# FFN weights transposed on TensorE instead of in a DMA, with a new order of VectorE's work beside the attention steps

## The chip, the cores and the metric

The kernel runs on one core of a Trainium2 chip. The metric is the device time of one execution in microseconds (us). Five engines work side by side, each through its own list of instructions in program order: TensorE (PE in the profile; its weight loads are PEld), VectorE (DVE), ScalarE (ACT), GpSimd (POOL) and SyncE (SP), which here only issues DMAs. They wait for one another on semaphores. TensorE writes into PSUM, of which this kernel uses eight banks of 128 x 512 float32.

## The reference

For each of four sequences of 512 rows and 512 columns, `x + s * g` is computed. `xn` is the layer norm of x. `s` is causal attention on xn with 16 heads of 32 columns; q and k get an RMS norm and a rotary embedding. `g` is silu of a gated FFN on xn with 1408 hidden columns, whose weights are integers less a zero point, times a scale for each row:

```python
def _qlinear(x, wq, scale):
    W = (wq.astype(jnp.float32) - ZERO_POINT) * scale[:, None]      # ZERO_POINT = 128
    return jnp.einsum('bsd,hd->bsh', x, W)

xn = _layernorm(x)
s = attention(xn, w_qkv, w_out, q_gamma, k_gamma)                   # 16 heads, causal
gate = silu(_qlinear(xn, wq_gate, s_gate))                          # wq_gate, wq_up: 1408 x 512
up = _qlinear(xn, wq_up, s_up)
g = silu(_qlinear(gate * up, wq_down, s_down))                      # wq_down: 512 x 1408
x = x + s * g
```

## The kernel before, in words

There is no scheduler: the order in which the Python code calls the instructions is the order on each engine. Work goes in 16 units (b, g): sequence b from 0 to 3, group of four heads g from 0 to 3. A unit has two stages.

`hidden_window` computes a chunk of the FFN: two 128-column pieces f in g = 0, three in the others. For each piece `hidden` makes the gate and the up product (16 matmuls of 512 columns; xn is split into two float32r halves, `xh` and `xl`), `gate` and `gated` apply silu and scales. Between them stand, as `fills`, leftovers of the unit before: its last attention step, and `fresh.turn`, which transposes the queries and keys of this unit on TensorE (tile `qkt`, L422).

The second stage is attention. A `Step` t handles queries t*128 to t*128+127: `scores` on TensorE (tile `sc`, L452), `probabilities` (for each of four heads a minimum on VectorE, L473, and an exponential on ScalarE, L483), a transpose of the result, and `values` (L539). Beside it run: the contraction of the FFN chunk with w_down (`contract`, `contract_two`, tile `dn`), the projections of the next unit (`fresh.product`, tile `qkv`, L370) and their rotation (`fresh.rotate`: `square` on ScalarE with the copy of v, three multiplications and a sum on VectorE, L402 to L409, then four operations on GpSimd, L410 to L412, the first being the sum qk + qs).

The stage has two forms. `attention_window` (units (0,0) to (0,2)) transposes the probabilities on TensorE (tile `pt`, L499). `placed_window` (the 12 units (0,3) to (3,2)) transposes them in 32 x 32 blocks on VectorE (`blocks`, L521) and puts these in place with four DMAs on SP (`spread`). In `placed_window` of g = 0 the output products of the sequence before are made too (`result.project`, tile `so`, L678, and `result.finish`), and q of the next unit's first tile is projected early, into a bank of the other pool. In g = 3 the next sequence's xn is split into halves: `norm.cut(t)` rounds on ScalarE (L352) and subtracts on GpSimd or VectorE (L353).

PSUM pools, in rings: `bank_a` has four banks (scores, qkv, h, so), `bank_t` two (transposes, one dn, some qkv and h), and one each hold `pv` and `dn`. A tile of a ring is free once its last reader is done.

The integer weights (34 pieces, 128 x 512 or 128 x 384) are prepared during units (0,0) to (0,2), two in each call of `weights()`: a load on SP (L247), a cast to bfloat16 on ScalarE (L256), a DMA transpose on SP (L258), and on VectorE the zero point's subtraction into float32r with a running maximum (L265). `weights()` is called behind each piece f of `hidden_window` and four times in each `attention_window`. `prologue` prepares the first four pieces. The pieces lie in `rooms`, memory that is used for other things later.

Of the kernel before, what the change touches and what calls it, by code (L numbers as in the profile page):

```python
# [13 lines left out]
BF16 = mybir.dt.bfloat16  # L14
U32 = mybir.dt.uint32
I32 = mybir.dt.int32
AF = mybir.ActivationFunctionType
ALU = mybir.AluOpType
# [3 lines left out]
P = 128  # L22
# [3 lines left out]
NT = N // P  # L26
NC = D // P
# [5 lines left out]
ZERO_POINT = 128.0  # L33
# [18 lines left out]
def interleaved(  # L52
# [27 lines left out]
    nc = tc.nc  # L80
# [23 lines left out]
    def bank_t(name):  # L104
        return ps_t.tile([P, 512], F32, tag="t", name=name)
# [37 lines left out]
    ident = const.tile([P, P], F32, name="ident")  # L143
# [41 lines left out]
    def load_scales():  # L185
# [5 lines left out]
            at += n  # L191
        return srow, at

    sdown = const.tile([P, D], F32, name="sdown")

    def prepare_scales(srow, at):
        tp = bank_t("sps")
# [32 lines left out]
    todo = list(preparations())  # L230
    n_prep = len(todo)
    largest = const.tile([P, n_prep], F32, name="largest")
    loaded, turning, finished = [], [], set()

# [2 lines left out]
    now = [0]  # L239
# [7 lines left out]
                nc.sync.dma_start(raw.bitcast(U32), src.bitcast(U32))  # L247
                loaded.append((now[0], room, raw, k, dst, name))

    def turn_weights():  # L250


        _, room, raw, k, dst, name = loaded.pop(0)
        halves_ = raw.bitcast(BF16)
        n = k * P
        nc.scalar.copy(halves_[:, :n], raw.bitcast(U32))  # L256
        turned = halves_[:, n:].rearrange("p (c r) -> p c r", r=P)
        nc.sync.dma_start(turned, halves_[:, :n], transpose=True)  # L258
        turning.append((now[0], room, turned, k, dst, name))

    def finish_weights():

        _, room, turned, k, dst, name = turning.pop(0)
        i = len(finished)
        nc.vector.tensor_scalar(  # L265
            dst,
            turned,
            -ZERO_POINT,
            None,
            ALU.add,  # L270
            ALU.max,
            accum_out=largest[:, i : i + 1],
        )
        if len(finished) >= NC:
            rooms.append(room)
        finished.add(name)

    def weights(n=2):

        now[0] += 1  # L280
        for _ in range(n):
            if turning and now[0] - turning[0][0] >= 2:
                finish_weights()
        load_weights(n)
        for _ in range(n):
            if loaded and now[0] - loaded[0][0] >= 1:
                turn_weights()

    def find_wide():

# [69 lines left out]
    class Projection:  # L360
# [16 lines left out]
            self.banks[t] = bank  # L377

        def square(self, t):
            bank = self.banks[t]  # L380
            nc.scalar.activation(squares, bank[:, : 2 * P], AF.Square)  # L381
            nc.scalar.copy(self.v[:, t, :], bank[:, 2 * P :])  # L382

        def rotate(self, t, squared=False):


            bank = self.banks[t]
            name = f"{self.b}_{self.g}_{t}"
            if not squared:
                self.square(t)  # L390
            qk = qp.tile([P, 2 * P], F32, tag="qk", name=f"qk_{name}")
            qs = tp_.tile([P, 2 * P], F32, tag="qs", name=f"qs_{name}")

            def four(a):
                return a.rearrange("p (i h d) -> p i h d", i=2, d=HD)

            def table(k, cols):
                a = tab[:, t, :, k, cols]
                return a.unsqueeze(2).to_broadcast([P, 2, HPG, a.shape[-1]])

            bank4 = four(bank[:, : 2 * P])
            nc.vector.tensor_tensor(four(qk), bank4, table(0, slice(0, HD)), ALU.mult)  # L402
            for lo, hi in ((0, half), (half, 0)):
                lo, hi = slice(lo, lo + half), slice(hi, hi + half)
                nc.vector.tensor_tensor(  # L405
                    four(qs)[:, :, :, lo], bank4[:, :, :, hi], table(1, lo), ALU.mult
                )
            ss = small.tile([P, 2 * HPG], F32, tag="ss", name=f"ss_{name}")
            nc.vector.tensor_reduce(ss, heads(squares), AX.X, ALU.add)  # L409
            nc.gpsimd.tensor_tensor(qk, qk, qs, ALU.add)  # L410
            inverse_root(ss, ss, HD * RMS_EPS)
            nc.gpsimd.tensor_tensor(  # L412
                heads(qk), heads(qk), ss.unsqueeze(2).to_broadcast([P, 2 * HPG, HD]), ALU.mult
            )
            self.qk[t] = qk
# [15 lines left out]
    class Step:  # L431
# [79 lines left out]
        def blocks(self, *js):  # L511

            n = self.t + 1
            used = HPG * self.keys
            probs = piece(self.first, n)[:, :used].rearrange("p (m k c) -> p c m k", c=4, k=32)
            way = piece(self.way, n)[:, :used].rearrange("p (c m k) -> p c m k", c=4, k=32)
            for j in js[:: self.per]:
                blocks = slice(j * n, (j + self.per) * n)  # L520
                nc.vector.transpose(way[:, :, blocks], probs[:, :, blocks])  # L521
# [302 lines left out]
    def placed_window(b, g, last, s, fresh, norm, result):  # L824

        def halves(engine, *tiles):
            if norm is not None:
                for t in tiles:  # L830
                    norm.cut(t, engine)

        def beside(t):
            if result is not None:
                result.project(t)
                result.finish(t)

        def load(*tiles):
            if result is not None:
                for t in tiles:  # L840
                    result.load(t)

        def values():
            for t in range(NT - 1):
                s[t].values()

        load(0)
        s[0].scores()
        s[1].scores(s[0].whole, s[0].keys)
        s[0].probabilities(0, 1, 2, 3)  # L850
        if g == 0:
            fresh.product(0, other=True)
            fresh.square(0)
        adds = contract_two(b, g)
        s[1].probabilities(0, 1, 2, 3)
        adds[0]()
        if g == 0:
            fresh.rotate(0, squared=True)
        if last.placed:
            last.values()  # L860
        s[2].scores()
        adds[1]()
        if g == 0:
            last.divide()
        s[0].blocks(0, 1, 2, 3)
        s[0].spread()
        s[2].probabilities(0, 1, 2, 3)
        add = contract(b, g, 2)
        s[2].blocks(0, 1, 2, 3)
        s[2].spread()  # L870
        if g:
            fresh.product(0)
            fresh.rotate(0)
        s[1].blocks(0, 1, 2, 3)
        s[1].spread()
        load(1, 2)
        if g == 0:
            add()
        halves(nc.gpsimd, 0, 1)
        for t in range(NT):  # L880
            if t:

                fresh.product(t, other=t == NT - 1 or (g > 0 and t == NT - 2))
                fresh.rotate(t)
            if t == 1 and g:
                add()
                last.divide()
            if t == 1:
                halves(nc.vector, 2, 3)
            beside(t)  # L890
            if t == 1:
                load(3)
        if g == 0:
            values()
        s[3].scores()
        s[3].probabilities(0, 1, 2, 3)
        contract(b, g, 3)()
        if g:
            values()
# [67 lines left out]
    def prologue():  # L967
        norm, fresh = Norm(0), Projection(0, 0)
        load_weights(4)
        scales_in = load_scales()  # L970
        load_weights(4)
        for t in range(NT):
            norm.stats(t)
            norm.roots(slice(t, t + 1))
            if t:
                norm.apply(t - 1)
                norm.turn(t - 1)
        norm.apply(NT - 1)
        prepare_table()
        norm.cut(0, nc.vector)  # L980
        norm.cut(1, nc.vector)
        fresh.product(0)
        fresh.rotate(0)
        norm.turn(NT - 1)
        norm.cut(2, nc.vector)
        norm.cut(3, nc.vector)
        load_weights(3)
        for _ in range(4):
            turn_weights()
        fresh.product(1)  # L990
        fresh.rotate(1)
        for _ in range(4):
            turn_weights()
        for t in range(2, NT):
            fresh.product(t)
            fresh.rotate(t)
            finish_weights()
            finish_weights()
        load_wqkv(slice(1, 2))
        now[0] += 1  # L1000
        prepare_scales(*scales_in)
        return fresh

    fresh, last, norm, done = prologue(), None, None, None
    for u, (b, g) in enumerate(units):
# [17 lines left out]
                done.store(t)  # L1023
        if (b, g) == (0, NC - 1):
            next(finding)
            nc.sync.dma_start(wout, w_out.rearrange("(c p) m -> p c m", p=P))
        if b == 0 and 2 + g < NC:
            load_wqkv(slice(2 + g, 3 + g))
        if (b, g) == (0, 0):
            nc.sync.dma_start(sdown, s_down.partition_broadcast(P))  # L1030
        if (b, g) == (0, NC - 2):
            finding = find_wide()
            next(finding)
# [485 lines left out]
```

## Time and profile before

| | |
|---|---|
| three runs, us | 658.75, 659.25, 659.99 (median 659.25) |
| profiled execution, us | 656.71, of which 654.9 are the span from first to last instruction |
| mean granted TensorE clock | 0.992 |
| busy, share of the span | PE 95%, DVE 74%, ACT 53%, POOL 48% |
| DMA transposes | 34, on SP |
| attention stage of (2,0) begins | 342.83 us (first `sc`) |
| attention stage of (2,1) begins | 393.11 us |

In the profile a line such as `PE so L678 <- DVE least L473: 6.6, 3, 2.2` says that TensorE's products `so` waited for VectorE's `least` for 6.6 us in all, three times, 2.2 us the longest. In a timeline the first two numbers are start and duration in us, `x8` is the number of instructions merged into the line, and brackets give the idle time before it and what ended that. `PEclk` is the share of full speed that TensorE was granted. The three units (1,0), (2,0) and (3,0) are alike, and so are (0,3), (1,3) and (2,3).

### The profile page before, as it was taken

What the parts mean: (1) busy time and instruction counts of PE and PEld (TensorE: products, weight loads), DVE (VectorE), ACT (ScalarE), POOL (GpSimd) and SP (SyncE); (2) the same over time, 40 slices, a digit from 0 to 9 for tenths busy, and PEclk for the clock granted to TensorE, in tenths of its full rate; (3) what the DMA queues carried; (4) which work ended last, traced back from release to release, by engine and by line L of the source; (5) the groups of instructions that cost most, each with busy time, mean ns of one, the idle gap of its engine ahead of it and who ended that gap; (6) DMA issues with size and microseconds to landing.
All of it is one profiled execution on the core that took longest, in us unless ns stands there. A gap on an engine that the chain in (4) does not pass through costs nothing.

```text
span 654.9 us, 11673 instructions
## 1 busy us (share of the span) xinstructions
PE 622.2 (95%) x3906; PEld 413.7 (63%) x3906; DVE 482.4 (74%) x1248; ACT 346.3 (53%) x895; POOL 317.0 (48%) x365
## 2 busy tenths in 40 slices
PE   4989999999988999999998999999997999999995
PEld 3646757667564576758664476767765467676752
DVE  4677776755988479797998369799798657969553
ACT  2666765646473264546755046464756136464560
POOL 3925235352563626544382633637194442727422
PEclk9999999999999999999998999999999899999999
DMA  8594853100433146243323425523233505333401
GB/s 267 144 215 110 185 133 101 66 1 1 98 82 87 59 130 162 66 96 66 79 44 81 121 48 144 137 61 83 65 80 82 145 1 146 82 73 89 130 1 70
DMA packets 65584, 62.63 MB, mean 96 GB/s; under 512 B 22998, under 2 KB 48876, under 8 KB 65516
## 3 DMA queue, kind: packets, MB, share of 16 engines
q1 hardware_dynamic: 64556, 61.38, 37.7%
q8 instruction: 33, 0.54, 0.3%
q10 hardware_dynamic: 960, 0.43, 0.2%
q14 instruction: 35, 0.29, 0.1%
HBM read 21.80 MB, written 4.19 MB: 40 GB/s over the span
## 4 chain that ended last, share of the span: by engine, by line
PE 79%; DVE 12%; ACT 4%; issue 2%; DMA 2%; POOL 0%; DVEq 0%; ACTq 0%
PE h L585 22%; PE qkv L370 21%; PE so L678 9%; PE sc L452 5%; PE dn L632 5%; PE dn L615 5%; PE pv L539 5%; DVE arena L521 3%; PE pt L499 2%; DVE arena L473 2%; PE qkt L422 2%; DVE qs L405 1%; PE rt L563 1%; ACT arena L483 1%; PE xnt L346 1%
## 5 line engine op out<-in xcount | busy, mean ns | idle before, releaser
L370 PE MATMUL qkv<-wqkv,xnT 128*128 128x384 f32 x512 | 172.5, 490 | 2.3 <-DVE least L473 2.3
L483 ACT ACTIVATE arena<-arena,least 128x128 f32<-128x128 f32 (+3 forms) x256 | 140.6, 551 | 63.4 <-DVE least L473 63.2
L370 PEld LDWEIGHTS qkv<-wqkv,xnT 128*128 128x128 f32 x512 | 96.3, 191 | 69.0 <-issue 4.2
L521 DVE STREAM_TRANSPOSE arena<-arena 128x512 f32<-128x512 f32 (+1 forms) x132 | 126.1, 1002 | 0.0
L410 POOL TENSOR_TENSOR qk<-qk,qs 128x256 f32<-128x256 f32 x64 | 48.2, 753 | 156.0 <-DVE qs L405 156.0
L473 DVE CUSTOM_DVE_ANT_0 arena<-sc,mask 128x128 f32<-128x128 f32 (+3 forms) x256 | 109.3, 485 | 15.1 <-PE sc L452 13.8
L604 POOL TENSOR_TENSOR h<-sil,h 128x512 fp32r<-128x512 f32 x44 | 57.9, 1315 | 110.5 <-ACT h L603 110.5
L317 POOL TENSOR_TENSOR ss<-ss,minus_half 128x8 f32<-128x8 f32 x64 | 106.9, 1671 | 5.3
L381 ACT ACTIVATE squares<-qkv 128x256 f32<-128x256 f32 x64 | 24.5, 383 | 122.5 <-PE qkv L370 98.0
L602 DVE SCALAR_TENSOR_TENSOR sil<-h,scales,sil 128x512 f32<-128x512 f32 x44 | 32.7, 743 | 52.6 <-PE h L585 43.7
L678 PE MATMUL so<-wout,oT 128*128 128x512 f32 x128 | 61.9, 625 | 6.6 <-DVE least L473 6.6
L603 ACT CAST h<-sil 128x512 fp32r<-128x512 f32 x44 | 27.3, 620 | 72.3 <-DVE sil L602 72.3
L402 DVE TENSOR_TENSOR qk<-qkv,tab 128x256 f32<-128x256 f32 x64 | 26.4, 412 | 44.7 <-ACT v L382 44.3
L632 PE MATMUL dn<-wdT,h 128*128 128x512 f32 x208 | 59.0, 419 | 0.0
L632 PEld LDWEIGHTS dn<-wdT,h 128*128 128x128 f32 x208 | 36.9, 188 | 25.8 <-issue 16.0
L585 PE MATMUL h<-xh,wuT 128*128 128x512 f32 x176 | 50.0, 406 | 1.7 <-ACT qT L125 1.7
L585 PE MATMUL h<-xh,wgT 128*128 128x512 f32 x176 | 50.0, 406 | 0.7 <-ACT v L382 0.7
L452 PE MATMUL sc<-kT,qT 32*128 32x512 f32 (+3 forms) x512 | 48.8, 467 | 1.4 <-DVE wdT L265 1.4
L585 PE MATMUL h<-xl,wgT 128*128 128x512 f32 x176 | 48.2, 395 | 0.0
L585 PE MATMUL h<-xl,wuT 128*128 128x512 f32 x176 | 48.1, 395 | 0.0
L483 ACT ACTIVATION_READ_ACCUMULATOR arena<-arena,least 128x1 f32 x256 | 47.9, 187 | 0.0
L678 PEld LDWEIGHTS so<-wout,oT 128*128 128x128 f32 x128 | 24.7, 199 | 33.9 <-issue 23.6
(92 smaller groups left out, 920.7 us busy)
## 6 DMA issues: line engine op xcount, KB each, us to landing
arena<-arena SPq DMA_DIRECT2D x48, 256.0 KB, 4.8
arena<-arena SPq DMA_DIRECT2D x48, 192.0 KB, 3.6
arena<-arena SPq DMA_DIRECT2D x48, 128.0 KB, 3.2
x<-in_L_attn_x SPq DMA_DIRECT2D x16, 256.0 KB, 4.3
out<-o SPq DMA_DIRECT2D x15, 256.0 KB, 4.4
wqkv<-in_L_attn_w_qkv SPq DMA_DIRECT2D x16, 192.0 KB, 3.4
arena<-arena SPq DMA_DIRECT2D x48, 64.0 KB, 2.1
xr<-in_L_attn_x SPq DMA_DIRECT2D x12, 256.0 KB, 3.8
```

The lines of the kernel that those rows point to most:

```text
L317: nc.gpsimd.tensor_tensor(dst, dst, minus_half[:, : dst.shape[-1]], ALU.pow)
L370: nc.tensor.matmul(bank.rearrange("p (i d) -> p i d", i=3), lhsT=xnT[:, c, ts(t, P)], rhs=wqkv[:, c, :, self.g, :], start=(c == 0), stop=( ...
L410: nc.gpsimd.tensor_tensor(qk, qk, qs, ALU.add)
L452: nc.tensor.matmul(bank, lhsT=qT[rows, ts(self.t, P)], rhs=kT[rows, : self.keys], start=True, stop=True,)
L473: nc.vector.tensor_tensor_reduce(out=pr, in0=self.banks[j], in1=mask[:, N - self.keys :], scale=float(HD), scalar=3.0e38, op0=ALU.add, op1 ...
L483: nc.scalar.activation(pr, pr, AF.Exp, bias=least, scale=-1.0, accum_out=self.sums[:, self.t, j : j + 1],)
L521: nc.vector.transpose(way[:, :, blocks], probs[:, :, blocks])
L539: nc.tensor.matmul(self.pv[j * HD : (j + 1) * HD, ts(self.t, P)], lhsT=self.v[:, k, ts(j, HD)], rhs=self.turned[j][:, k], start=(k == 0), ...
L585: nc.tensor.matmul(bank, lhsT=w[:, c, ts(f, P)], rhs=a[:, c, :], start=(c == 0 and a is xh), stop=(c == NC - 1 and a is xl),)
L604: nc.gpsimd.tensor_tensor(to[:, 1, :], sil, to[:, 0, :].bitcast(F32), ALU.subtract)
L632: nc.tensor.matmul(bank, lhsT=h[:, i, a, ts(t, P)], rhs=wdT[:, f, :], start=(i == 0 and a == 0), stop=(f == fs[-1] and a == 1),)
L678: nc.tensor.matmul(self.banks[t], lhsT=oT[:, g, ts(t, P)], rhs=wout[:, g, :], start=(g == 0), stop=(g == NC - 1),)
```

## The change

It has three parts.

1. The DMA transposes go. The cast piece is transposed on TensorE in 128 x 128 blocks of bfloat16, two pieces into one `bank_t` bank, and VectorE subtracts the zero point from PSUM. The cast comes one call of `weights()` later than before. The bfloat16 identity lies in the memory of `sdown`, so that `sdown` is loaded in unit (0,3) instead of (0,0).
2. In `placed_window` of g = 0, the minima of step 2 come ahead of the blocks of step 0 and of the rotation of tile 0; the copy of v for tile 0 is a method of its own (`keep`) and comes after the exponentials of step 2.
3. In `placed_window` of g = 3, all four cuts stand at the head of the stage, with their subtractions on GpSimd; the blocks of step 0 come behind the minima of step 2; and the sum qk + qs of the last tile is made on VectorE.

For g = 1 and g = 2 the order of `placed_window` stays as it was.

```diff
+    ident16 = sdown[:, : P // 2].bitcast(BF16)
+    nc.gpsimd.tensor_copy(ident16, ident)
...
-    def turn_weights():
...
-        nc.scalar.copy(halves_[:, :n], raw.bitcast(U32))
-        turned = halves_[:, n:].rearrange("p (c r) -> p c r", r=P)
-        nc.sync.dma_start(turned, halves_[:, :n], transpose=True)
...
+    def cast_weights():
...
+        narrow = raw.bitcast(BF16)[:, : k * P]
+        nc.scalar.copy(narrow, raw.bitcast(U32))
+        cast.append((now[0], room, narrow, k, dst, name))
+
+    def turn_weights(n=2):
...
+        bank = bank_t(f"wt_{len(finished)}").bitcast(BF16)
+        for i in range(n):
+            _, room, narrow, k, dst, name = cast.pop(0)
+            turned = bank[:, i * 4 * P : (i * 4 + k) * P]
+            for c in range(k):
+                nc.tensor.transpose(turned[:, ts(c, P)], narrow[:, ts(c, P)], ident16)
+            at = len(finished)
+            nc.vector.tensor_scalar(
+                dst,
+                turned.rearrange("p (c r) -> p c r", r=P),
...
     def weights(n=2):
 
         now[0] += 1
-        for _ in range(n):
-            if turning and now[0] - turning[0][0] >= 2:
-                finish_weights()
+        ready = [c for c in cast[:n] if now[0] - c[0] >= 1]
+        if ready:
+            turn_weights(len(ready))
         load_weights(n)
         for _ in range(n):
-            if loaded and now[0] - loaded[0][0] >= 1:
-                turn_weights()
+            if loaded and now[0] - loaded[0][0] >= 2:
+                cast_weights()
...
-            nc.gpsimd.tensor_tensor(qk, qk, qs, ALU.add)
+            adder.tensor_tensor(qk, qk, qs, ALU.add)
...
+        if norm is not None:
+            for t in range(NT):
+                norm.cut(t)
         load(0)
         s[0].scores()
...
         adds[0]()
-        if g == 0:
-            fresh.rotate(0, squared=True)
         if last.placed:
             last.values()
         s[2].scores()
         adds[1]()
         if g == 0:
             last.divide()
-        s[0].blocks(0, 1, 2, 3)
-        s[0].spread()
+        elif norm is None:
+            blocks(0)
         s[2].probabilities(0, 1, 2, 3)
         add = contract(b, g, 2)
-        s[2].blocks(0, 1, 2, 3)
-        s[2].spread()
-        if g:
+        if g == 0:
+            blocks(0)
+            fresh.rotate(0, squared=True)
+            fresh.keep(0)
+            blocks(2, 1)
+            add()
+        else:
+            if norm is not None:
+                blocks(0)
+            blocks(2)
             fresh.product(0)
             fresh.rotate(0)
-        s[1].blocks(0, 1, 2, 3)
-        s[1].spread()
+            blocks(1)
         load(1, 2)
-        if g == 0:
-            add()
-        halves(nc.gpsimd, 0, 1)
         for t in range(NT):
             if t:
...
-                fresh.rotate(t)
+                fresh.rotate(t, adder=nc.vector if norm is not None and t == NT - 1 else nc.gpsimd)
...
-            if t == 1:
-                halves(nc.vector, 2, 3)
             beside(t)
```

More of the change, by code (lines that the diff above doesn't have):

```diff
@@ L232, in interleaved @@
     largest = const.tile([P, n_prep], F32, name="largest")
-    loaded, turning, finished = [], [], set()
+    loaded, cast, finished = [], [], set()
     rooms = [piece(i) for i in range(NC)]
@@ L248, in load_weights @@
                 loaded.append((now[0], room, raw, k, dst, name))
-    def turn_weights():
+    def cast_weights():
         _, room, raw, k, dst, name = loaded.pop(0)
-        halves_ = raw.bitcast(BF16)
-        n = k * P
-        nc.scalar.copy(halves_[:, :n], raw.bitcast(U32))
-        turned = halves_[:, n:].rearrange("p (c r) -> p c r", r=P)
-        nc.sync.dma_start(turned, halves_[:, :n], transpose=True)
[L259 to L276, printed above, removed]
+        narrow = raw.bitcast(BF16)[:, : k * P]
[12 more added lines that the diff above has]
+                turned.rearrange("p (c r) -> p c r", r=P),
+                -ZERO_POINT,
+                None,
+                ALU.add,
+                ALU.max,
+                accum_out=largest[:, at : at + 1],
+            )
+            if at >= NC:
+                rooms.append(room)
+            finished.add(name)
     def weights(n=2):
         now[0] += 1
-        for _ in range(n):
-            if turning and now[0] - turning[0][0] >= 2:
-                finish_weights()
+        ready = [c for c in cast[:n] if now[0] - c[0] >= 1]
+        if ready:
+            turn_weights(len(ready))
         load_weights(n)
         for _ in range(n):
-            if loaded and now[0] - loaded[0][0] >= 1:
-                turn_weights()
+            if loaded and now[0] - loaded[0][0] >= 2:
+                cast_weights()
     def find_wide():
@@ L379, in square, with keep, rotate @@
         def square(self, t):
[L380 to L384, printed above, removed]
+            nc.scalar.activation(squares, self.banks[t][:, : 2 * P], AF.Square)
+        def keep(self, t):
+            nc.scalar.copy(self.v[:, t, :], self.banks[t][:, 2 * P :])
+        def rotate(self, t, squared=False, adder=nc.gpsimd):
             bank = self.banks[t]
@@ L390, in rotate @@
                 self.square(t)
+                self.keep(t)
             qk = qp.tile([P, 2 * P], F32, tag="qk", name=f"qk_{name}")
@@ L824, in placed_window, with blocks @@
     def placed_window(b, g, last, s, fresh, norm, result):
[L828 to L831, printed above, removed]
+        def blocks(*ts_):
+            for t in ts_:
+                s[t].blocks(0, 1, 2, 3)
+                s[t].spread()
         def beside(t):
@@ L988, in prologue @@
         for _ in range(4):
-            turn_weights()
+            cast_weights()
         fresh.product(1)
@@ L992, in prologue @@
         for _ in range(4):
-            turn_weights()
+            cast_weights()
         for t in range(2, NT):
@@ L996, in prologue @@
             fresh.rotate(t)
-            finish_weights()
-            finish_weights()
+            turn_weights()
         load_wqkv(slice(1, 2))
@@ L1025, in interleaved @@
             next(finding)
+            nc.sync.dma_start(sdown, s_down.partition_broadcast(P))
             nc.sync.dma_start(wout, w_out.rearrange("(c p) m -> p c m", p=P))
@@ L1028, in interleaved @@
             load_wqkv(slice(2 + g, 3 + g))
-        if (b, g) == (0, 0):
-            nc.sync.dma_start(sdown, s_down.partition_broadcast(P))
         if (b, g) == (0, NC - 2):
```

## The prediction

> **What bounds the kernel now.** I read the page first, then the list of waits, and then timelines of the stages that the longest waits of TensorE point to.
>
> ```profile
> PE 622.2 (95%) x3906; PEld 413.7 (63%) x3906; DVE 482.4 (74%) x1248; ACT 346.3 (53%) x895; POOL 317.0 (48%) x365
> PE 79%; DVE 12%; ACT 4%; issue 2%; DMA 2%; POOL 0%; DVEq 0%; ACTq 0%
> ```
>
> TensorE is busy 95% of the span and 79% of the chain that ended last. So an added TensorE instruction costs its time wherever TensorE doesn't stand still, and a gain elsewhere counts only where TensorE waits. The list of waits:
>
> ```profile
> PE so L678 <- DVE least L473: 6.6, 3, 2.2
> PE qkt L422 <- POOL qk L412: 2.6, 3, 1.3
> PE h L585 <- ACT qT L125: 1.7, 3, 0.6
> ACT wout L256 <- DMA wout<-in_L_ffn_wq_up: 2.6, 2, 1.5
> ```
>
> Three waits of 2.2 us are the output products, one in each unit with g = 0 from (1,0) on. The next two rows are three waits each, around the turn of q and k behind a g = 3 stage. Unit (2,0), TensorE's timeline, then VectorE's:
>
> ```profile
> 349.33 0.93 PE L452 MATMUL sc<-kT,qT 32*128 32x384 f32 x8
> 350.19 1.20 PE L632 MATMUL dn<-wdT,h 128*128 128x512 f32 x4
> 353.59 5.40 PE L678 MATMUL so<-wout,oT 128*128 128x512 f32 x8 [2.20 <-DVE least L473]
> ```
>
> ```profile
> 349.77 0.42 DVE L402 TENSOR_TENSOR qk<-qkv,tab 128x256 f32<-128x256 f32 x1 [1.04 <-ACT v L382]
> ...
> 350.83 0.68 DVE L646 COPY acc<-dn 128x512 f32<-128x512 f32 x1
> 351.43 0.68 DVE L568 TENSOR_TENSOR oT<-pv,rT 128x512 f32<-128x512 f32 x1
> 352.03 1.07 DVE L521 STREAM_TRANSPOSE arena<-arena 128x512 f32<-128x512 f32 x1
> 353.02 0.52 DVE L473 CUSTOM_DVE_ANT_0 arena<-sc,mask 128x384 f32<-128x384 f32 x1
> ```
>
> The product needs a bank that the first minimum at 353.02 frees. Ahead of that minimum stand the rotation (with 1.04 us of waiting for ScalarE's v) and one block. After the wait the same product is slow too: 5.40 us for 8, where the chain has 3.43 in the next. The windows say why (the seventh column is the granted clock):
>
> ```profile
> 345.00:352.00 7.00, 6.39 (x57) 3.87 (x55) 4.67 (x19) 6.10 (x21) 1.84 (x4) 1.00 0.29 84
> 352.00:359.00 7.00, 5.41 (x9) 2.37 (x10) 7.00 (x16) 2.50 (x8) 2.04 (x2) 0.76 0.17 37
> ```
>
> ```profile
> 353.59 5.40 PE so L678 x8
> ...
> 361.57 3.43 PE so L678 x8
> ```
>
> **Part 1, weights on TensorE.** Removed: 34 DMA transposes on SP, for which TensorE is not seen waiting. Casts stay 34. VectorE's 34 subtractions stay, from PSUM instead of SBUF: the nearest row with a PSUM source is the copy of kT, 0.67 us, against 0.68 now, so nothing (bounds -1 to +2 us). Added on TensorE: 34 pieces of 4 blocks less 4 x 1 (the last four have 3), 132 transposes with as many weight loads. No row shows a bfloat16 transpose; the nearest are the float32 ones of the same shape, from the chain, and the clock beside them:
>
> ```profile
> 68.37 0.87 PE qkt L422 x8
> 61.00:76.00 15.00, 15.00 (x105) 12.46 (x107) 9.16 (x24) 8.97 (x16) 7.77 (x9) 1.00 0.82 200
> ```
>
> That is 0.109 us each, so 14.4 us at most. From below: L585 streams 512 float32r columns in 1.87 us for 8 (0.234 each), which for 128 columns is 0.058, or 7.7 us in all. The Trainium skill ("TensorE: Matmul & The Clock Gate", section "Back-to-back issue gap") gives about 0.081 us for a stream of loads and matmuls of 128 columns, 10.7 us; it lies between the two and I take it. The same page speaks against the change ("Part 4: PE-mode transpose"): some 0.275 us in a kernel, and no credit with the clock gate. That would be 36 us. The rows above don't agree: 0.109 us, at a clock of 1.00.
>
> What of 10.7 us is exposed? Walking through the stages:
> - Prologue and the two pieces of unit (0,0), 32 blocks, 2.6 us: hidden. The two late casts of that stage (36.11 us, behind 1.11 us of waiting for a load) hold up the exponentials until 38.05; with the cast one call later this one leaves the place, so the exponentials can start as soon as their minima are there. The minima move back by some 2 us (from 35.5 to 37.4: two groups of blocks, and the last two subtractions now wait behind the bank that qT frees), so tile 0's four exponentials are done at about 39.4 us as before.
> - Attention stage of (0,0), four groups of 8 blocks, 0.65 us each: two lie in TensorE's gaps of 0.62 and 0.74 us ahead of `qkv`. The third also waits about 0.45 us for a `bank_t` bank that ScalarE must still empty (its pt copy is some 0.5 us). 0.65 x 2 + 0.45 = 1.75.
> - Unit (0,1): seven groups, 4.55 us. The first stands directly behind two `pt` groups whose VectorE copy has yet to come (h's product 0.75 us, then the copy, ready at 67.00 where TensorE is free at 66.35): 0.7 us more; 0.45 more in the attention stage as above; gaps of 0.47 and 0.44 us hide 0.9. Together 4.8.
> - Unit (0,2): 12 blocks, 1.0 us, and the 0.7 us of bank wait: 1.7.
>
> Exposed: 1.75 + 4.8 + 1.7 = 8.2 us. At 0.058 us a block it is about 6.3, at 0.109 about 12, with nothing hidden 14.4 + 2.3 = 16.7. The load of `sdown` moves on SP to (0,3), near 158 us; its first reader (L663) runs at 188.6. The identity's copy on GpSimd falls into the 6 us before x lands. Both cost nothing.
>
> **Part 2, g = 0, three times.** Rotation and block leave the place ahead of the minima. In (2,0): sum of dn ends at 348.73, the second 0.6 later, then the division 0.7 (pv's matmuls are done at 349.4), so the minimum ends near 350.7, while TensorE is free at 351.4. The wait of 2.2 us goes. With it goes the slow clock: 5.40 - 3.43 = 1.97 us in (2,0) and the same in (3,0) (5.40 there as well), 3.70 - 3.43 = 0.27 in (1,0). Here a rule and the trace differ. The skill (same page, "Part 1: The HAM clock gate") has the clock fall after an idle window of about 3.4 us, so 2.2 us would cost no clock and the part would bring 3 x 2.2 = 6.6 us. The row has 0.76 behind 2.2 us; I follow it: 6.6 + 1.97 + 1.97 + 0.27 = 10.8 us.
>
> What is moved back: the rotation's three products and reduction on VectorE, its four operations on GpSimd (from 350.7 to about 354; GpSimd's next work is at 361.2), the copy of v behind step 2's exponentials (its reader `values` comes near 376), the four DMAs of step 0's spread on SP (same reader). The bank of the projection stays taken until about 354.5; the next claim on that ring is the last `qkv`, over 10 us later. VectorE's total up to the sum of dn (359.89) does not grow. Later TensorE finds VectorE waiting for it (1.66 us ahead of L691 at 365.04, 2.51 ahead of L402 at 368.25), so the gain isn't handed back there.
>
> **Part 3, g = 3, three times.** Where TensorE stands (end of (1,3)):
>
> ```profile
> 337.86 0.49 PE L422 MATMUL qkt<-ident,qk 128*128 128x128 f32 x3
> 339.00 0.76 PE L422 MATMUL qkt<-ident,qk 128*128 128x128 f32 x5 [0.65 <-POOL qk L412]
> 340.33 1.20 PE L585 MATMUL h<-xh,wuT 128*128 128x512 f32 x4 [0.57 <-ACT qT L125]
> ```
>
> GpSimd is without a pause from 322.16 to 338.9: four rotations of 3.35 us and two cuts of 1.47. Without these cuts and one sum (0.75) it ends about 3 us earlier. But qT's copy on ScalarE is also behind VectorE's `sil` at 337.86 and two activations. VectorE loses two cuts, 2.4 us (326.51 to 328.92), and gains a sum of about 0.4. Against that, four casts of 0.575 us now stand ahead of the exponentials: step 2's end at 321.5 instead of 319.2, and the blocks of step 2 at 322.4 instead of 321.25, 1.15 us lost. Net 0.9 us of the 1.22. In (0,3) VectorE had started later and loses nothing to the casts: 1.35 of its 1.90. Together 3.1 us; bounds: 4.3 (all six waits), and a loss of 3 (each stage late by 1 us because the casts hold up more than that). GpSimd's cuts at the head find it idle for 9.79 us.
>
> **The sum** is made against the profiled execution: 656.7 + 8.2 - 10.8 - 3.1 = 651.0. It lay 2.5 us below the median of the runs shown, 659.25; on that median it is 653.6 us.
>
> **Rivals.** (a) TensorE has no room in units (0,0) to (0,2): each block takes the 0.109 us of float32 and nothing of it is hidden, since the wait for one of two `bank_t` banks takes the place of the old gaps. 16.7 - 13.9 = +2.8, 662 us. It decides from an exposed 13.9 us on. For: two banks, whose readers are VectorE and ScalarE. Against: the gaps before the change, and half the width. (b) The casts at the head hold up exponentials, blocks and rotation in g = 3 by more than the cuts gave: part 3 loses 3. 8.2 - 10.8 + 3 = +0.4, 659.7 us. For: ScalarE has no pause from 312 to 319. Against: VectorE has the minima in between. (c) In g = 0 the wait goes but the clock falls anyway: part 2 gives 6.6, the sum is -1.5, 657.7 us. Against: clock 1.00 in every other stage without such a gap.
>
> **How the numbers follow.** Forecast 0.60, (a) 0.20, (b) 0.10, (c) 0.10. About 0.2% (1.3 us) is what can be told from no change. Faster: the forecast but for a small tail, and half of (c): 0.64. Same: (b)'s larger half and the rest of (c): 0.12. Slower: (a) and what is left: 0.24. The likeliest case by itself spans 650 to 657; the range goes from 648.5 (blocks at 0.058 us, all of part 3) to 661.5, which leaves out the upper half of (a).
>
> **What would show it.** Right: no wait of `so` for `least`; eight `so` in 3.4 us and a clock near 1.00 in all three g = 0 stages; eight `wt` transposes in 0.5 to 0.9 us; unit (0,1) longer by 4 to 6 us. Wrong: `wt` groups waiting over 1 us for VectorE or ScalarE; minima or blocks of a g = 3 stage waiting for `arena` of ScalarE for over 2 us; a new wait of `so` for oT.

## The result and the profile after

The changed kernel takes 685.33 us (median of four runs, 683.95 to 687.05), against 659.0 before: 1.041 times as long, 95% interval 1.037 to 1.045. The forecast was 653.6 us with a range up to 661.5. The profiled execution took 684.19 us with a span of 682.4. From its page, the engines' busy time and the chain that ended last:

```profile
PE 631.3 (93%) x4038; PEld 422.6 (62%) x4038; DVE 480.0 (70%) x1245; ACT 346.1 (51%) x895; POOL 320.8 (47%) x369
PE 87%; DVE 6%; ACT 4%; issue 1%; DMA 1%; SPq 0%; DVEq 0%; ACTq 0%
```

TensorE has 9 us more of busy time (622.2 before), the span has 27.5 us more. Most of the loss is thus time in which TensorE does nothing. The list of waits names it:

```profile
PE wt L268 <- DVE wgT L270: 20.7, 10, 3.1
PE wt L268 <- DVE wdT L270: 6.4, 5, 2.8
PE wt L268 <- ACT h L610: 2.6, 2, 1.3
...
PE h L592 <- ACT qT L125: 2.2, 3, 0.8
```

The weights' transposes (`wt`) waited for VectorE's subtractions of the zero point: 27.1 us in 15 waits. With the two waits of the third row these are 17, one for each group of two pieces, and 29.7 us. (In these two the subtraction ended within 0.1 us of the ScalarE cast that the list names, so they belong to the same kind.) The rows of `so` waiting for `least` and of `qkt` waiting for GpSimd, which stood there before, are gone; the wait for qT is still there, 2.2 us where it was 1.7. One group, in the attention stage of (0,0), on TensorE and on VectorE:

```profile
57.26 2.75 PE L375 MATMUL qkv<-wqkv,xnT 128*128 128x384 f32 x8
59.84 0.39 PE L268 MATMUL wt<-sdown,oT 128*128 128x128 bf16 x4
62.48 0.59 PE L268 MATMUL wt<-sdown,wout 128*128 128x128 bf16 x4 [2.25 <-DVE wgT L270]
```

```profile
60.68 0.43 DVE L409 TENSOR_TENSOR qk<-qkv,tab 128x256 f32<-128x256 f32 x1 [1.66 <-ACT v L388]
61.02 0.48 DVE L412 TENSOR_TENSOR qs<-qkv,tab 128x128 f32<-128x128 f32 x2
61.41 0.41 DVE L416 TENSOR_REDUCE ss<-squares 128x8 f32<-128x256 f32 x1
61.74 0.68 DVE L270 TENSOR_SCALAR_CACHE_REDUCE wgT<-wt 128x512 fp32r<-128x512 bf16 x1
...
63.10 0.69 DVE L270 TENSOR_SCALAR_CACHE_REDUCE wuT<-wt 128x512 fp32r<-128x512 bf16 x1 [0.68 <-PE wt L268]
```

The first piece's four transposes run at once. The second piece's four lie in the other half of the same PSUM bank and start at 62.48, when the first piece's subtraction has ended. That subtraction stands on VectorE behind the rotation, which waits for ScalarE, which waited for TensorE's `qkv`. In the changed program the first transpose of each second piece waits for a semaphore of VectorE. The two engines take turns twice: VectorE in its turn waits 0.68 us for the second piece.

The product that part 2 was for, unit (2,0), TensorE's timeline and then the window of the whole stage (clock in the seventh column):

```profile
385.91 1.20 PE L639 MATMUL dn<-wdT,h 128*128 128x512 f32 x4
386.95 3.60 PE L685 MATMUL so<-wout,oT 128*128 128x512 f32 x8
```

```profile
378.55:424.67 46.12, 46.12 (x254) 28.47 (x253) 31.12 (x76) 19.77 (x52) 22.51 (x24) 1.00 0.38 92
```

TensorE is busy for the whole of the stage, 46.12 us of 46.12, at full clock. And behind the g = 3 stage of (1,3):

```profile
374.22 1.04 PE L429 MATMUL qkt<-ident,qk 128*128 128x128 f32 x8
376.05 1.20 PE L592 MATMUL h<-xh,wuT 128*128 128x512 f32 x4 [0.79 <-ACT qT L125]
```

The eight transposes run in one stretch; the wait for qT stays and is 0.79 instead of 0.57 us.

Stage by stage, from the start of one attention stage (first `sc`) to that of the next, in us, with three of the kernels below beside them:

| stretch | before | after | transposes of both pieces first | DMA transposes, parts 2 and 3 | the same, sum on GpSimd |
|---|---|---|---|---|---|
| start to (0,3) | 158.71 | 199.08 | 165.00 | 159.06 | 158.70 |
| (0,3) | 32.31 | 30.79 | 30.62 | 31.41 | 30.94 |
| (1,3), (2,3) | 32.54, 32.51 | 31.89, 31.90 | 31.89, 31.90 | 31.91, 31.90 | 31.99, 31.77 |
| (1,0) | 48.60 | 46.12 | 46.12 | 46.13 | 46.13 |
| (2,0), (3,0) | 50.28, 50.38 | 46.12, 46.13 | 46.13, 46.12 | 46.12, 46.13 | 46.12, 46.12 |

The preparation of the weights costs 40.4 us, the two new orders give back 13.7. The remaining 0.8 us of the span's 27.5 lie behind these stages.

### The profile page after: what moved, and what is told of

It reads as the page before. It is cut to its first block, busy times and chain, and to the rows that moved or that the text cites. A ratio compares the mean times of both kernels' runs of the same rounds, so it can differ in the third digit from the quotient of the medians.

```text
span 682.4 us, 11843 instructions
## 1 busy us (share of the span) xinstructions
PE 631.3 (93%) x4038; PEld 422.6 (62%) x4038; DVE 480.0 (70%) x1245; ACT 346.1 (51%) x895; POOL 320.8 (47%) x369
## 4 chain that ended last, share of the span: by engine, by line
PE 87%; DVE 6%; ACT 4%; issue 1%; DMA 1%; SPq 0%; DVEq 0%; ACTq 0%
PE h L592 24%; PE qkv L375 23%; PE so L685 8%; PE dn L639 8%; PE sc L459 7%; PE pv L546 5%; PE dn L622 5%; PE pt L506 2%; PE qkt L429 2%; PE wt L268 1%; PE rt L570 1%; DVE wgT L270 1%; ACT arena L490 1%; DVE sil L609 1%; PE xnt L351 1%
## 5 line engine op out<-in xcount | busy, mean ns | idle before, releaser
L375 PE MATMUL qkv<-wqkv,xnT 128*128 128x384 f32 x512 | 174.6, 494 | 0.0
L417 POOL TENSOR_TENSOR qk<-qk,qs 128x256 f32<-128x256 f32 x61 | 44.5, 729 | 167.2 <-DVE qs L412 167.2
L685 PE MATMUL so<-wout,oT 128*128 128x512 f32 x128 | 58.1, 593 | 0.0
L639 PEld LDWEIGHTS dn<-wdT,h 128*128 128x128 f32 x208 | 37.4, 192 | 25.0 <-issue 13.7
L546 PE MATMUL pv<-arena,v 128*32 128x128 f32 x1280 | 44.6, 279 | 0.1
```

What stands on the lines that cost most here:

```text
L375: nc.tensor.matmul(bank.rearrange("p (i d) -> p i d", i=3), lhsT=xnT[:, c, ts(t, P)], rhs=wqkv[:, c, :, self.g, :], start=(c == 0), stop=( ...
L417: adder.tensor_tensor(qk, qk, qs, ALU.add)
L546: nc.tensor.matmul(self.pv[j * HD : (j + 1) * HD, ts(self.t, P)], lhsT=self.v[:, k, ts(j, HD)], rhs=self.turned[j][:, k], start=(k == 0), ...
L639: nc.tensor.matmul(bank, lhsT=h[:, i, a, ts(t, P)], rhs=wdT[:, f, :], start=(i == 0 and a == 0), stop=(f == fs[-1] and a == 1),)
L685: nc.tensor.matmul(self.banks[t], lhsT=oT[:, g, ts(t, P)], rhs=wout[:, g, :], start=(g == 0), stop=(g == NC - 1),)
```

## The experiments

My theory A was the shared bank, with VectorE's queue behind it. Rivals were B, that the transposes themselves are dear (their number, their weight loads, the clock), and C, that the ring of two banks is.

**Transposes of both pieces first.** Only the order within a group changes:

```diff
+        both = []
         for i in range(n):
...
                 nc.tensor.transpose(turned[:, ts(c, P)], narrow[:, ts(c, P)], ident16)
+            both.append((turned, room, dst, name))
+        for turned, room, dst, name in both:
             at = len(finished)
             nc.vector.tensor_scalar(
```

> The changed kernel, but in each group the transposes of both pieces come first and the two subtractions after them, so that TensorE never writes a bank that VectorE is reading in the same group. Theory A (what is dear is the second piece's wait for VectorE, because both pieces lie in one PSUM bank): the 27.1 us of waits of wt for VectorE's subtraction go, VectorE waits some 0.3 us longer for each group; 685.3 - 27 to 30 = 655 to 658 us. Theory B (the transposes themselves, their weight loads and the clock are dear): at most 3 us less than 685. Theory C (the ring of two banks is dear: the groups wait for the bank of an earlier tile): the waits move to the first piece of each group, less than 8 us gained.

Measured: 649.86 us (649.1 to 650.02), 0.987 of the kernel before, interval 0.985 to 0.989. That is 35.5 us less than the changed kernel, by nothing but this order. TensorE no longer waits for a subtraction within a group; what is left are five waits of a group's first piece for its bank, 2.7 us:

```profile
L268 PE MATMUL wt<-sdown,wout 128*128 128x128 bf16 x70 | 5.8, 220 | 1.4 <-DVE kT L127 0.8 <-ACT arena L125 0.6
L268 PE MATMUL wt<-sdown,oT 128*128 128x128 bf16 x46 | 3.9, 219 | 1.3 <-DVE arena L127 1.3
L268 PE MATMUL wt<-sdown,arena 128*128 128x128 bf16 x16 | 1.2, 219 | 0.0
```

(In the list by lines, the numbers behind the first bar are busy time and mean ns, behind the second the idle time and its causes.) The gain is 5 us larger than theory A had expected. Slower products account for about that much. Up to (0,3) TensorE was busy for 157.94 us in the changed kernel and for 151.92 here, with the same instructions, and the mean clock was 0.97 there and is 1.00 here.

```profile
0.00:199.08 199.08, 157.94 (x1034) 110.14 (x1034) 106.80 (x311) 93.69 (x226) 74.78 (x98) 0.97 0.27 79
```

```profile
0.00:165.00 165.00, 151.92 (x1035) 107.10 (x1035) 104.53 (x311) 93.59 (x226) 74.66 (x98) 1.00 0.31 95
```

The first window is of the changed kernel, the second of this one. The 0.97 comes from three stretches of 3.41 us in which the changed kernel was granted half the clock (from 24.71, 62.26 and 120.29 us). They explain at most 3 x 3.41 x 0.5 = 5.1 of the 6.0 us; the rest was not traced.

**A bank for each piece**, in the order of the change:

```diff
-        bank = bank_t(f"wt_{len(finished)}").bitcast(BF16)
         for i in range(n):
+            bank = bank_t(f"wt_{len(finished)}").bitcast(BF16)
...
-            turned = bank[:, i * 4 * P : (i * 4 + k) * P]
+            turned = bank[:, : k * P]
```

> The changed kernel with its order, but each of the two pieces of a group in a bank of its own from the same ring of two. Theory A (sharing a bank): the second piece no longer waits for the subtraction of the first; it waits for the tile that held the second bank before, which is mostly read by then: 15 to 27 us less than 685, so 658 to 670 us, behind the order of transposes first because each group takes the whole ring. Theory B (transposes themselves): no change. Theory C (the ring is dear): slower than 685.

Measured: 654.42 us (654.03 to 655.48), 30.9 less than the changed kernel, a larger gain than expected. Most groups now run through, and no `wt` wait is longer than 0.8 us:

```profile
44.67 0.61 PE L268 MATMUL wt<-sdown,oT 128*128 128x128 bf16 x8
```

The subtraction still stands between the two pieces in the program, and the long waits are gone: it takes the bank in common to make them. The ring of two is no bar: taking the whole ring costs 4.6 us against the order above. Theories B and C fall. In these kernels each bank is also one tile of the program, and no run tells a shared tile from a shared bank.

**Each block transposed twice**, on top of "both pieces first":

```diff
+            for _ in range(2):
                 for c in range(k):
                     nc.tensor.transpose(turned[:, ts(c, P)], narrow[:, ts(c, P)], ident16)
```

> As the kernel with both pieces' transposes first, but every weight block is transposed twice into the same place, 132 more transposes. It measures the price of one: at 0.058 us a block 7.7 us more than that kernel, at 0.081 10.7, at 0.109 14.4, less what still lies in gaps of TensorE. Theory B wants over 14 us.

Measured: 655.31 us, 5.45 us more for 132 more transposes, 0.041 us each. The three rows of `wt` add up to 18.2 us of busy time here and 10.9 there, 0.055 each. That is half of the float32 transposes' 0.109 and under the 0.081 that I had taken. (A single record lasts 0.22 us; the records of a run overlap.)

**The preparation as before, both new orders kept.** The functions of part 1 are those of the kernel before, all else is the changed kernel's.

> The changed kernel with the weights prepared as before the change (DMA transposes); only the parts for g = 0 and g = 3 are left. By the stages of the two traces these give 2.5 + 4.2 + 4.2 us (g = 0) and 1.5 + 0.65 + 0.6 us (g = 3), 13.7 together: 659.0 - 13.7 = 645.3 us, ratio 0.979. If the gains of these stages lean on what the weights did before them (an earlier or later start of VectorE), it is under 10 us.

Measured: 644.4 us (644.13 to 645.2), 0.979, interval 0.977 to 0.981. The gains of parts 2 and 3 don't lean on part 1. Against it, the repaired part 1 still costs 5.5 us (649.86 to 644.4), 5.9 by the first row of the table.

**Part 2 alone**, on the kernel before:

```diff
-        if g == 0:
-            fresh.rotate(0, squared=True)
...
-        s[0].blocks(0, 1, 2, 3)
-        s[0].spread()
+        else:
+            blocks(0)
         s[2].probabilities(0, 1, 2, 3)
         add = contract(b, g, 2)
...
+        if g == 0:
+            blocks(0)
+            fresh.rotate(0, squared=True)
+            fresh.keep(0)
+            blocks(2, 1)
+            add()
...
```

> The kernel before with the new order of the g = 0 stage alone (minima ahead of block and rotation). The forecast's sum for this part was 10.8 us, 6.6 of them idle time and 4.2 the slower clock behind it: 658.5 - 10.8 = 647.7 us, with every g = 0 stage at 46.1 us (48.6, 50.3 and 50.4 before) and no clock under 1.00 there. If the clock had fallen for another reason than the wait: 658.5 - 6.6 = 651.9 us.

Measured: 647.97 us (645.48 to 648.96), 0.982, interval 0.979 to 0.984, 11.3 us less than its runs of before (659.27); the g = 0 stages are 46.1 us each at clock 1.00. This agrees with 10.8 and not with the 6.6 us expected if the slow clock had another reason than the wait. The profiled execution shows the slow clock elsewhere, behind the stage of (0,3), in a place that part 2 leaves alone:

```profile
187.98 0.76 PE L425 MATMUL qkt<-ident,qk 128*128 128x128 f32 x5 [1.40 <-POOL qk L415]
189.27 2.04 PE L588 MATMUL h<-xh,wuT 128*128 128x512 f32 x4 [0.52 <-ACT qT L125]
```

```profile
189.00:193.40 4.40, 4.13 (x16) 3.14 (x16) 2.43 (x4) 1.48 (x3) 1.54 (x2) 0.61 0.76 127
```

The same two waits, 1.35 and 0.55 us, stood there before and brought no slow clock (the last section shows the difference).

**Only the block moved**, so that half of the wait of `so` stays:

```diff
-        s[0].blocks(0, 1, 2, 3)
-        s[0].spread()
+        if g:
+            s[0].blocks(0, 1, 2, 3)
+            s[0].spread()
         s[2].probabilities(0, 1, 2, 3)
         add = contract(b, g, 2)
+        if g == 0:
+            s[0].blocks(0, 1, 2, 3)
+            s[0].spread()
```

> The kernel before, with only the block of step 0 moved behind the minima in g = 0; the rotation stays ahead of them. The wait of the output product shrinks by the block's 1.0 us to about 1.2 us. If the clock follows the length of the idle time, it stays at 1.00 in all three stages, eight products take 3.4 to 3.7 us, and the gain is 3 x 1.0 + 4.2 = 7.2 us: 651.3. If any wait of about a microsecond brings the slow clock, the products stay at 5.4 us in (2,0) and (3,0) and the gain is 3.0 us: 655.5.

Measured: 650.92 us (649.9 to 653.26), 8.4 us less than before; expected were 7.2 if the clock follows the length of the idle time. In (2,0):

```profile
352.12 3.70 PE L678 MATMUL so<-wout,oT 128*128 128x512 f32 x8 [1.25 <-DVE least L473]
```

A wait of 1.25 us is left in each of the three stages, and in none is the clock under 1.00. So at the same place a shorter wait leaves the clock alone. The length is not all that counts: in (1,0) of the kernel before, the full 2.21 us brought no slow clock either (last section). By the stages of the two profiles this order gained 6.4 us; the profile of the kernel before is one of its faster executions, 656.71 against 659.27.

**The last tile's sum back on GpSimd**, on the kernel with DMA transposes and both orders:

```diff
-                fresh.rotate(t, adder=nc.vector if norm is not None and t == NT - 1 else nc.gpsimd)
+                fresh.rotate(t)
```

> The kernel with DMA transposes and both new orders (644.4 us), but the sum qk + qs of the last tile in g = 3 back on GpSimd. If VectorE's chain to the copy of qT sets the end there, as the forecast said, VectorE wins 0.4 us in each of three stages: 643.2 to 644.4 us, and qkt doesn't wait for GpSimd. If GpSimd's chain sets it, qkt waits for GpSimd again and the three stages are 0.3 to 0.7 us longer each: 645.3 to 646.5 us.

Measured: 643.09 us (642.73 to 644.17), 0.976, interval 0.974 to 0.978; `qkt` doesn't wait for GpSimd. The three g = 3 stages take 94.7 us together instead of 95.2. That is the first of the two outcomes named: VectorE's chain and not GpSimd's sets the end there, and moving the sum to VectorE bought nothing. The kernel with the sum on VectorE ran on another chip, and the two intervals touch, so I claim only that this one is no slower. It has the lowest time of this study and beats both kernels.

**The weights ahead of the rotation**, two pieces still in one bank:

```diff
         project(1)
-        rotate(1)
-        halves(2, 3)
         beside(1)
+        rotate(1)
+        halves(2, 3)
```

(and likewise for tiles 0, 2 and 3)

> The changed kernel, but in the attention stages of (0,0) to (0,2) the group of weights is prepared ahead of the rotation instead of behind it, so that VectorE's subtraction of the first piece does not stand behind the rotation (1.3 us and its wait for ScalarE). Two pieces still share a bank. Theory A says that the second piece then waits for the subtraction alone, 0.7 us instead of 2.2, in the seven groups that stood directly behind a projection: some 8 us of waits gone, of which the rotation takes back a part by coming later: 676 to 681 us against 685.3. If the wait is not made by VectorE's queue, nothing changes.

Measured: 674.85 us (673.13 to 676.45), 10.5 less than the changed kernel, a slightly larger gain than expected. The 17 waits sum to 20.6 us instead of 29.7. The second piece behind a projection:

```profile
60.98 0.39 PE L268 MATMUL wt<-sdown,oT 128*128 128x128 bf16 x4
62.16 0.38 PE L268 MATMUL wt<-sdown,wout 128*128 128x128 bf16 x4 [0.79 <-DVE wgT L270]
```

Beside the 2.25 us of the changed kernel, this splits the wait: about 0.8 us are the subtraction itself, the rest is the rotation ahead of it on VectorE.

## Why the prediction was wrong

**The step that failed is the walk of part 1, where each group of eight blocks was put down as one run of 0.65 us.** It put the wait between the two pieces of a group at nothing; the runs showed 29.7 us of it. I had weighed waits for a bank, but only at the first block of a group, for what an earlier tile had left there. That the second piece writes into the bank from which VectorE reads the first I passed over, though the diff shows both slices of one `bank`. The Trainium skill states the rule ("PSUM — Partial Sum Buffer", section "PSUM bank collisions raise a hardware error"): a write by TensorE and a read by another engine must not meet in one bank and 32-partition quadrant, even at other columns, and are to be guarded by bank and not by address. This rule should have been weighed against the order within a group. The trace agrees as far as it can: the program keeps the two accesses apart by waiting, 29.7 us in 17 waits. No run here shows what a collision would do.

What the 40.4 us to the stage of (0,3) are made of, against 8.2 forecast:

| | us | from |
|---|---|---|
| second pieces' waits | 29.7 | list of waits, 20.7 + 6.4 + 2.6 |
| first pieces' waits | 2.6 | timeline: 0.78, 0.29, 0.62, 0.29, 0.64 |
| 132 transposes | 7.5 | busy PE to (0,3): 151.92 with both pieces first, 144.37 with DMA transposes |
| slower products | 6.0 | busy PE to (0,3): 157.94, against 151.92 with both pieces first; at most 5.1 of it by the clock |
| waits of before that vanished | -5.4 | seven gaps between 23 and 96 us |

That the terms add up to 40.4 to the tenth is chance: among three of the kernels with DMA transposes the busy time up to (0,3) alone differs by 0.7 us (143.69 to 144.37).

The other terms of the walk held up. With both pieces first, the preparation costs 5.9 us. The walk at 0.058 us a block had said 6.3; at the 0.081 that I took, 8.2. The low estimate, made from the kernel's own rows, was the right one, and the waits for an earlier tile came out at 2.7 us (2.3 in the walk). The sum of the three parts would then have been 659.0 + 5.9 - 10.9 - 2.8 = 651.2, and the repaired kernel is near it: 649.86. So the order within a group is what separates the result from the forecast.

**Part 2** came out: 2.48 + 4.16 + 4.25 = 10.9 us by the table, forecast 10.8. Following the row of clock 0.76 rather than the rule of the Trainium skill ("TensorE: Matmul & The Clock Gate", section "Part 1: The HAM clock gate", an idle window of about 3.4 us) was right in size: 6.6 us would have been too little. A window of that length is in the traces too, but it need not be idle throughout (last section). How often the slow clock comes depends on where the waits fall, so the 4.2 us that it cost belong to this execution; in another it can be more or less.

**Part 3** came out at 1.5 + 0.65 + 0.6 = 2.8, forecast 3.1. The wait for GpSimd went as forecast. The wait for qT, behind ScalarE's activations, did not shrink: it holds TensorE up for 2.2 us in all, 1.7 before. With the sum back on GpSimd `qkt` did not wait either, so the cuts' new place and the blocks' new order carry this part, and the moved sum brought nothing. No run separates those two.

**The rivals.** (a) pointed to the right stage and the right kind of cause and ended on the right side, but its mechanism was the ring of two banks and transposes at float32's price; its 662 us are 23 us short. Neither (b) nor (c) happened. Of the signs that would show the forecast wrong, the first came: `wt` waiting over 1 us for VectorE. The range had a slip of its own: blocks at 0.058 us and all of part 3 give 659.25 + 6.3 - 10.8 - 4.3 = 650.5 for its lower end, not 648.5. That had no part in the miss.

## What to carry to other kernels

Two pieces in one PSUM bank took turns here as if they were one: fill the bank with everything first, and let the readers start after; when a bank is shared, look for the write that comes after a read. On an engine that works in program order, such a wait costs what stands ahead of the reader in its queue (here 2.25 us, of which the subtraction is 0.8). And what a waiting TensorE loses can be more than the wait, since half a clock may follow it.

## What the runs showed of the hardware

- **The slow clock comes in fixed stretches.** In these traces, whose record of the clock begins 13 to 16 us into an execution, the granted clock is either 1.00 or 0.50. Every slow stretch in which TensorE had work lasts 3.41 us; the 0.76 and 0.61 above are windows that hold one. Two stretches of one execution lie a whole multiple of 3.413 us apart: 153.60 us (45 times) in the kernel before, 37.55 and 58.03 us (11 and 17 times) in the changed one. So each execution has a raster of such windows.
- **What goes with them is how little TensorE worked in the window just before.** Two pairs of neighbouring windows, of (1,0) and of (2,0) in the kernel before:

```profile
197.84:201.25 3.41, 1.75 (x12) 0.68 (x5) 3.28 (x8) 2.07 (x9) 2.23 (x3) 1.00 0.00 0
201.25:204.67 3.42, 2.87 (x7) 1.44 (x8) 3.42 (x12) 2.50 (x8) 0.99 (x2) 1.00 0.28 61
351.44:354.86 3.42, 1.27 (x3) 0.68 (x4) 3.42 (x10) 1.55 (x7) 2.51 (x4) 1.00 0.09 19
354.86:358.27 3.41, 3.41 (x5) 1.33 (x4) 3.41 (x7) 1.22 (x5) 0.00 (x0) 0.50 0.26 58
```

  The wait is 2.2 us in both. In (2,0) nearly all of it lies in one window, TensorE is busy for 1.27 us of that, and the next window has half the clock. In (1,0) a border at 201.25 us cuts the wait in two, TensorE is busy for 1.75 us, and the clock stays. The nine slow stretches with work in the ten traces of this case followed windows with 0.40 to 1.49 us of work. Behind windows with 1.56 us or more none came. Two windows in between had none behind them either, with 1.40 us (a bank for each piece, at its end) and 1.46 us (the changed kernel, from 106.63), so the limit lies near 1.4 to 1.5 us of 3.41. This fits the two open cases above: with part 2 alone the window ahead of the slow stretch had 1.49 us of work, while in the kernel before a border fell between the same two waits (2.06 and 2.86 us); and a wait of 1.25 us by itself leaves more than 2 us of work in its window.
- **Transposes count as work for the clock.** In the changed kernel the window from 41.78 to 45.19 us has 1.84 us of work, of which about 1.5 are transposes, and the clock behind it is 1.00.
- The kernel before shows two slow stretches in its profile and a mean clock of 0.992. Most of its other executions have 0.989 or 0.990. One stretch more would lower the mean by 0.5 x 3.41 / 655 = 0.0026, so these may have had it in (1,0) too; they have no trace, and this is an estimate.
- A bfloat16 transpose of 128 x 128 in a run of eight takes 0.055 us of TensorE, half of a float32 one (0.109). Its weight load is hidden: 132 more transposes with as many loads added 5.45 us in all.
